# Softmax sums taken over halved keys, and a first convolution computed twice instead of kept

## The chip, the cores and the metric

The kernel runs on one core of a Trainium2 chip. The metric is the device time of one execution in microseconds (us). A core has five engines that run at the same time and wait for each other through semaphores: TensorE (PE in the profile, with its weight loads listed as PEld), VectorE (DVE), ScalarE (ACT), GpSimd (POOL) and SyncE (SP), which here issues the DMA transfers.

## The reference

Two layers are applied to x, four images of 128 channels and 128x128 pixels, all in fp32.

Layer 0 cuts each image into 9x9 overlapping regions of 16x16 pixels with a step of 14. Each region is normalised over the channels and goes through attention with 4 heads of 32 channels; the projected result is added to the region, and overlapping regions are averaged. What follows is a layer norm, a projection to 256 channels, a depthwise 5x5 convolution, a batch norm, two GELUs, a projection back to 128 channels and a residual. For one region and one head:

```
attn = softmax(q @ k.T * hd ** -0.5)     # 256 queries x 256 keys
o    = attn @ v
```

Layer 1 is a block of two 3x3 convolutions with activations and weights quantised to 4 bits:

```
out = act_quant(x)                         # clip to 0..1, round to 15 levels
out = conv3x3(out, weight_quant(w1)); out = batchnorm(out, gamma1, beta1)
out = act_quant(out)
out = conv3x3(out, weight_quant(w2)); out = batchnorm(out, gamma2, beta2)
return out + x
```

A batch norm takes its mean and variance over all four images, so a convolution has to be finished for all of them before any of its results can be normalised.

## The kernel before, in words

**Attention (lines 287 to 705).** A band is one row of 9 regions; there are 4 x 9 = 36 bands and 324 regions. The order of work on PE, ACT and VectorE is written out by hand: these three run their instructions in the order in which the program records them, while GpSimd's and SP's orders come from the scheduler. For region j of a band the loop records `scores(j)`, then `values` of the region before (kept in `last`), then half of the side steps due, then `values_in(j)`, then the other half.

`scores(j)` multiplies keys by queries, with the keys on the partitions (line 561), and takes the exponentials on ACT (line 569). Each of the two tiles `pt` holds two heads and two halves of the keys, 128 keys each, for 256 queries. `values(j)` multiplies them by v and, for the sums, by a matrix of ones; both are accumulated over the two halves (line 615). The reciprocal of the sums (line 628) and the products with it (lines 630, 632) are VectorE's; GpSimd adds the overlapping columns (line 635). An fp32 matmul appears as two rows in the profile, so that one region has 16 rows with v and 16 with ones.

The side steps belong to the band after (normalise and project to q and k: lines 306 to 318 and 382 to 389), to the band before (output projection line 420, residual `xf` line 423, second layer norm, projection line 437) and to the depthwise convolution of an earlier half image (line 496, its copy line 505, its statistics line 507). At a band's start GpSimd averages the overlaps (lines 404, 405, 407), which line 420 then reads. In `normalise`, ACT squares into the tile `sq` (line 308), PE averages it (line 313), and ACT makes `rstd` of it in two steps (lines 315, 316); VectorE multiplies (`xn`, line 318).

**First quantised convolution (lines 800 to 864).** This and the rest is ordered by the scheduler. A block is 4 rows of an image; there are 128. Each block loads the depthwise results `cv` and the residual `xfl` (two blocks ahead), applies batch norm and both GELUs on ACT (lines 841, 846), projects (line 849, four rows on PE), stores the layer's output `id_d`, and quantises it into the padded fp8 image `q1`. `first_conv` then convolves the block before it (line 787, nine matmuls), takes its statistics (line 794) and keeps the result: images 0 to 2 are copied to a tile and written to `c1_d` in memory (lines 829, 831), image 3 is copied to `c1_s` in SBUF.

**Second quantised convolution (lines 865 to 925).** When all statistics are there, a scale and a shift are made from them (on VectorE and, for the power at line 725, GpSimd). Then each block's first result is loaded again (line 881, two blocks ahead) or read from `c1_s`; ACT scales it (line 889), VectorE quantises it (lines 890, 891) into `q2`, which takes the buffers of `q1`, and the second convolution runs for its statistics alone. A last pass computes the second convolution again, scales it (line 918), adds the stored input and writes the output.

Of the kernel before, what the change touches and what calls it, by code (L numbers as in the profile page):

```python
# [8 lines left out]
F32 = mybir.dt.float32  # L9
F8 = mybir.dt.float8e4  # L10
AF = mybir.ActivationFunctionType
ALU = mybir.AluOpType
AX = mybir.AxisListType

P = 128
HEADS = 4
HD = P // HEADS
# [3 lines left out]
NT = RS * RS  # L21
RB = 4
# [19 lines left out]
def layers(  # L42
# [29 lines left out]
    nc = tc.nc  # L72
    B = x.shape[0]
# [14 lines left out]
    ]  # L88
    cv_d = [dram.tile([P // GR, 2 * P, GR * P], F32, name=f"cv_d{b}") for b in range(B)]
    dw_d = dram.tile([NCK, P, 16 * 3 * 32], F32, name="dw_d")  # L90

    c1_d = [dram.tile([P, P * P], F32, name=f"c1_d{b}") for b in range(B - 1)]
    id_d = [dram.tile([P, P * P], F32, name=f"id_d{b}") for b in range(B)]

    def vector(v, name):
# [191 lines left out]
    with ExitStack() as actx:  # L287
# [3 lines left out]
        xp, rp, yp, op = pool("xp", 4), pool("rp", 2), pool("yp", 2), pool("op", 2)  # L291
        y2p, up, cp = pool("y2p", 2), pool("up", 2), pool("cp", 2)
        work, att, attn_t = pool("work", 2), pool("att", 2 if safe else 4), pool("attn_t", 2 if safe else 3)
        small = pool("small", 6)
        ps_s, ps_o, ps_m = (pool(n, k, space=PSUM) for n, k in (("ps_s", 1), ("ps_o", 1), ("ps_m", 3)))

        xb, yr, qs, kr, ob = {}, {}, {}, {}, {}
# [1 line left out]
        def normalise(src, n):  # L299


            held = {}

            def head():
                pc = ps_m.tile([P, 512], F32, name="pm")
                nc.tensor.matmul(pc[:, :n], center, src(), start=True, stop=True)  # L306
                sq = work.tile([P, 512], F32, name="sq")
                nc.scalar.activation(sq[:, :n], pc[:, :n], AF.Square)  # L308
                held["sq"] = sq

            def tail():
                pv = ps_m.tile([P, 512], F32, name="pm")
                nc.tensor.matmul(pv[:, :n], avg, held["sq"][:, :n], start=True, stop=True)  # L313
                rstd = work.tile([P, 512], F32, name="rstd")
                nc.scalar.activation(rstd[:, :n], pv[:, :n], AF.Ln, bias=eps_t)  # L315
                nc.scalar.activation(rstd[:, :n], rstd[:, :n], AF.Exp, scale=-0.5)
                xn = work.tile([P, 512], F32, name="xn")
                nc.vector.tensor_tensor(xn[:, :n], src(), rstd[:, :n], ALU.mult)  # L318
                return xn

            return head, tail
# [209 lines left out]
        def attention(t):  # L531
# [24 lines left out]
            def scores(j):  # L556
# [10 lines left out]
                for p in range(2):  # L567
                    pt = att.tile([P, 2, 2, NT], F32, name="pt")
                    nc.scalar.activation(pt, sc[p], AF.Exp)  # L569
                    S["pt", j].append(pt)  # L570

            def scores_safe(j):
                S["pt", j] = [att.tile([P, 2, 2, NT], F32, name="pt") for p in range(2)]
                qt = attn_t.tile([P, NT], F32, name="rd")
                nc.vector.tensor_copy(
                    qt.rearrange("p (r c) -> p r c", c=RS), queries(j, slice(0, P))
                )
                for h in range(HEADS):
                    hs = slice(h * HD, (h + 1) * HD)
                    sc = ps_s.tile([P, 2, 2, NT], F32, name=f"sc{h % 2}")  # L580
                    for c in range(2):
                        nc.tensor.matmul(
                            sc[:, 0, c, :],
                            qt[hs, c * P : (c + 1) * P], region(kr, j)[hs],
                            start=True, stop=True,
                        )
                    nmax = small.tile([P, 2], F32, name="nmax")
                    nc.vector.tensor_reduce(nmax, sc[:, 0], AX.X, ALU.max, negate=True)
                    pr = attn_t.tile([P, 2, NT], F32, name="pr")
                    den = small.tile([P, 2], F32, name="den")  # L590
                    for c in range(2):
                        nc.scalar.activation(
                            pr[:, c, :], sc[:, 0, c, :], AF.Exp, bias=nmax[:, c : c + 1],
                            accum_out=den[:, c : c + 1],
                        )
                    nc.vector.reciprocal(den, den)
                    for c in range(2):
                        nc.gpsimd.tensor_scalar(
                            pr[:, c, :], pr[:, c, :], den[:, c : c + 1], 1.0, ALU.mult, ALU.mult
                        )  # L600
                    for kc in range(2):
                        for c in range(2):
                            nc.tensor.transpose(
                                sc[:, 1, kc, c * P : (c + 1) * P], pr[:, c, kc * P : (kc + 1) * P], ident
                            )
                    nc.scalar.copy(S["pt", j][h // 2][:, h % 2], sc[:, 1])

            def values(j):
                pt, v = S.pop(("pt", j)), S.pop(("v", j))
                po = ps_o.tile([P, 2, NT], F32, name="po")  # L610
                for m in range(1 if safe else 2):
                    for kc in range(2):
                        for h in range(HEADS):
                            hs = slice(h * HD, (h + 1) * HD)
                            nc.tensor.matmul(  # L615
                                po[hs, m, :], ones if m else v[:, kc, hs], pt[h // 2][:, h % 2, kc, :],
                                start=(kc == 0), stop=(kc == 1),
                            )
                o, po_ = ob[t], po[:, 0, :].rearrange("p (r c) -> p r c", c=RS)
                new = o[:, :, j * STEP + 2 if j else 0 : j * STEP + RS]  # L620
                part = attn_t.tile([P, RS, 2], F32, name="part")
                if safe:
                    nc.vector.tensor_copy(new, po_[:, :, 2 if j else 0 :])
                    if j:
                        nc.vector.tensor_copy(part, po_[:, :, 0:2])
                else:
                    rd = attn_t.tile([P, NT], F32, name="rd")
                    nc.vector.reciprocal(rd, po[:, 1, :])  # L628
                    rd_ = rd.rearrange("p (r c) -> p r c", c=RS)
                    nc.vector.tensor_tensor(new, po_[:, :, 2 if j else 0 :], rd_[:, :, 2 if j else 0 :], ALU.mult)  # L630
                    if j:
                        nc.vector.tensor_tensor(part, po_[:, :, 0:2], rd_[:, :, 0:2], ALU.mult)
                if j:
                    seam = o[:, :, j * STEP : j * STEP + 2]
                    nc.gpsimd.tensor_tensor(seam, seam, part, ALU.add)

            begin()
            return scores_safe if safe else scores, values_in, values

        def beside(t):  # L640

# [37 lines left out]
        with nullcontext() if safe else tc.manual_schedule(engines=MANUAL):  # L679
# [3 lines left out]
                    s()  # L683
            last = None
            for t in range(T):
                scores, values_in, values = attention(t)
                if t + 1 < T:
                    ln1_begin(t + 1)
                side, at = beside(t), 0
                for j in range(NR):  # L690
                    scores(j)
                    if last:
                        last()
                    if j == 0 and t:
                        post_begin(t - 1)
                    for half in range(2):
# [96 lines left out]
    def stats_of(st, n, pc):  # L793
        nc.vector.bn_stats(st[:, n, :], pc.rearrange("p r c -> p (r c)"))  # L794
# [2 lines left out]

    c1_s = q1p.tile([P, P * P], F32, name="c1_s")  # L800
    q1 = [padded(q1p, f"q1_{b}") for b in range(B)]
    with (
        tc.tile_pool(name="ld", bufs=3) as ld,
# [16 lines left out]
            nc.sync.dma_start(out=xf, in_=xf_d[b][:, px])  # L820
            loaded[n] = cv, xf

        def first_conv(n):
            b, k = blocks[n]
            px = slice(k * RB * P, (k + 1) * RB * P)
            pc = conv3x3(q1[b], wq[0], k)
            stats_of(st1, n, pc)
            o = bw.tile([P, RB * P], F32, name="c1") if b < B - 1 else c1_s[:, px]
            nc.scalar.copy(o, pc.rearrange("p r c -> p (r c)"))
            if b < B - 1:  # L830
                nc.sync.dma_start(out=c1_d[b][:, px], in_=o)

        load(0)
        load(1)
        for n, (b, k) in enumerate(blocks):
# [22 lines left out]
                a.rearrange("p (r c) -> p r c", c=P), ROUND, None, ALU.subtract, saturate=False,  # L858
            )
            if k:  # L860
                first_conv(n - 1)
            if k == NBLK - 1:
                first_conv(n)

    sc1, sh1 = batchnorm([st1], 1, ga1, be1, kscale[0], "1")
    nc.vector.tensor_scalar(sc1, sc1, 15.0, None, ALU.mult)
    nc.vector.tensor_scalar(sh1, sh1, 15.0, None, ALU.mult)


    q2 = [padded(q1p, f"q1_{b}") for b in range(B)]  # L870
    ew = ctx.enter_context(tc.tile_pool(name="ew", bufs=3))
    firsts = {}

    def load_first(n):
        b, k = blocks[n]
        px = slice(k * RB * P, (k + 1) * RB * P)
        if b == B - 1:
            firsts[n] = c1_s[:, px]
            return
        firsts[n] = ew.tile([P, RB * P], F32, name="c1l")  # L880
        nc.sync.dma_start(out=firsts[n], in_=c1_d[b][:, px])

    load_first(0)
    load_first(1)
    for n, (b, k) in enumerate(blocks):
        if n + 2 < len(blocks):
            load_first(n + 2)
        a = ew.tile([P, RB * P], F32, name="a")
        nc.scalar.activation(a, firsts.pop(n), AF.Relu, bias=sh1, scale=sc1)
        nc.vector.tensor_scalar(a, a, 15.0, ROUND, ALU.min, ALU.add)  # L890
        nc.vector.tensor_scalar(
            q2[b][:, 1 + k * RB : 1 + (k + 1) * RB, 1 : 1 + P],
# [77 lines left out]
```

## Time and profile before

| what | value |
|---|---|
| three runs | 4054.0, 4057.53 and 4063.75 us; median 4057.53 |
| profiled execution | 4057.53 us; span of its instructions 4055.7 us |
| granted TensorE clock, mean | 0.973 |
| PE busy | 3762.9 us (93%), 35916 rows |
| VectorE busy | 1826.5 us (45%) |
| ScalarE busy | 2326.4 us (57%) |
| GpSimd busy | 384.2 us (9%) |
| DMA | 643.68 MB, 159 GB/s over the span |

The span runs from the first to the last instruction of one profiled execution; its own time has 1.8 us more around it. Busy time is the union of an engine's rows. Matmuls are pipelined: a row lasts from its start to the modelled end of its result, and the next one can start before that. The granted clock is the share of full speed that PE was given. A release, written `<-`, names what ended an engine's idle time.

### The profile page before, as it was taken

To read this page: it belongs to the slowest core of one execution; us is meant where nothing else is said; L and a number is where in the kernel's file an instruction comes from. 1 tells how busy PE (TensorE), PEld (TensorE's weight loads), DVE (VectorE), ACT (ScalarE), POOL (GpSimd) and SP (SyncE) were. 2 spreads that over 40 slices of the span, in tenths; PEclk is the share of its full clock that TensorE was granted. 3 is DMA by queue.
4 is the path that set the end of the run, shared out by engine and by line. 5 is a ranking of instruction groups with operands and counts; after the bars stand their busy time and mean duration, and the time that the engine had idled before them with its cause. 6 is when DMAs were issued, how large, how long until landed. Compare 5 with 4: busy or idle time off the path is not lost.

```text
span 4055.7 us, 87210 instructions
## 1 busy us (share of the span) xinstructions
PE 3762.9 (93%) x35916; PEld 1914.1 (47%) x35916; DVE 1826.5 (45%) x3358; ACT 2326.4 (57%) x3534; POOL 384.2 (9%) x1381
## 2 busy tenths in 40 slices
PE   7699999999999999999999999997688889999999
PEld 5355455555555555555545555553333333334444
DVE  5244444444444444444444444442245555685433
ACT  3367666666666666666666666653156667662233
POOL 0011110111110010111110111100011111100000
PEclk9999999999999999999999999998579999999999
DMA  1223266676656657655666764657888889760487
GB/s 39 108 62 80 73 135 149 146 143 152 148 116 141 148 134 159 150 140 110 150 147 139 160 146 118 144 129 162 182 255 300 295 297 304 231 199 1 137 271 250
DMA packets 782938, 643.68 MB, mean 159 GB/s; under 512 B 572736, under 2 KB 585664, under 8 KB 782528
## 3 DMA queue, kind: packets, MB, share of 16 engines
q1 hardware_dynamic: 782528, 637.98, 60.8%
q8 instruction: 286, 4.69, 0.5%
q14 instruction: 124, 1.02, 0.1%
HBM read 365.07 MB, written 272.76 MB: 157 GB/s over the span
## 4 chain that ended last, share of the span: by engine, by line
PE 76%; DMA 9%; ACT 4%; issue 3%; DVE 3%; POOL 2%; SPq 2%; ACTq 0%; POOLq 0%; DVEq 0%
PE po L615 14%; PE pc L787 12%; PE pm L496 9%; PE sc L561 8%; PE pm L306 6%; PE pm L382 6%; PE pm L313 6%; PE pm L437 5%; DMA cv<-cv_d 3%; PE pm L549 3%; PE pb L849 3%; PE pm L420 2%; PE pw L269 2%; DMA c1l<-c_d 2%; DMA u<-y_d 2%
## 5 line engine op out<-in xcount | busy, mean ns | idle before, releaser
L628 DVE RECIPROCAL rd<-po 128x256 f32<-128x256 f32 x324 | 569.6, 1758 | 633.4 <-PE po L615 633.4
L787 PE MATMUL pc<-q,wq 128*128 128x512 fp8e4 x3456 | 794.5, 382 | 23.3 <-DVE st L794 9.4
L569 ACT ACTIVATE pt<-sc 128x1024 f32<-128x1024 f32 x648 | 627.2, 1019 | 58.0 <-PE sc L561 47.1
L787 PEld LDWEIGHTS <-wq 128*128 128x128 fp8e4 x3456 | 337.4, 98 | 517.5 <-issue 151.6
L496 PE MATMUL pm<-u,w 40*32 40x256 f32 x12288 | 454.6, 410 | 57.4 <-DMA u<-y_d 44.7
L507 DVE BATCH_NORM_STATS2 st<-c 128x6 f32<-128x256 f32 x512 | 181.4, 414 | 469.4 <-ACT c L505 468.9
L561 PE MATMUL sc<-q,kr 32*128 32x256 f32 x5184 | 373.6, 401 | 0.0
L496 PEld LDWEIGHTS pm<-u,w 40*32 40x32 f32 x12288 | 258.7, 112 | 240.8 <-issue 112.2
L505 ACT COPY c<-pm 128x512 f32<-128x512 f32 x256 | 139.0, 588 | 386.8 <-PE pm L496 377.8
L615 PE MATMUL po<-pt,v 128*32 128x256 f32 x5184 | 346.9, 385 | 0.0
L615 PE MATMUL po<-pt,ones 128*32 128x256 f32 x5184 | 339.1, 379 | 0.0
L561 PEld LDWEIGHTS sc<-q,kr 32*128 32x128 f32 x5184 | 233.9, 184 | 218.7 <-issue 181.3
L313 PE MATMUL pm<-sq,avg 128*128 128x512 f32 (+1 forms) x576 | 281.9, 571 | 31.7 <-ACT sq L308 27.0
L443 ACT ACTIVATE y<-pm,bp 128x512 f32<-128x512 f32 (+1 forms) x288 | 183.4, 641 | 222.9 <-PE pm L437 111.9
L849 PE MATMUL pb<-ge,wp 128*128 128x512 f32 x512 | 265.6, 614 | 46.6 <-ACT ge L846 46.5
L382 PE MATMUL pm<-xn,wqkv 128*128 128x512 f32 (+1 forms) x576 | 269.2, 570 | 15.6 <-DVE xn L318 15.6
L437 PE MATMUL pm<-xn,wp 128*128 128x512 f32 (+1 forms) x576 | 268.9, 559 | 5.7 <-DVE xn L318 5.7
L841 ACT ACTIVATE ge<-cv,shift,scale 128x512 f32<-128x512 f32 x256 | 202.8, 844 | 111.2 <-DMA cv<-cv_d 107.2
L308 ACT ACTIVATE sq<-pm 128x512 f32<-128x512 f32 (+1 forms) x288 | 157.2, 546 | 187.8 <-PE pm L306 187.7
L794 DVE BATCH_NORM_STATS2 st<-pc 128x6 f32<-128x512 f32 x256 | 177.8, 696 | 189.3 <-PE pc L787 189.2
L918 ACT ACTIVATE z<-pc,shift,scale 128x512 f32<-128x512 f32 x128 | 99.3, 777 | 269.0 <-PE pc L787 130.1
L315 ACT ACTIVATE rstd<-pm,eps_t 128x512 f32<-128x512 f32 (+1 forms) x288 | 184.3, 640 | 120.3 <-PE pm L313 114.7
(143 smaller groups left out, 4026.0 us busy)
## 6 DMA issues: line engine op xcount, KB each, us to landing
u<-y_d SPq DMA_DIRECT2D x128, 528.0 KB
cv_d<-c SPq DMA_DIRECT2D x512, 128.0 KB
cv<-cv_d SPq DMA_DIRECT2D x128, 512.0 KB
y_d<-y SPq DMA_DIRECT2D x224, 264.0 KB
w<-dw_d SPq DMA_DIRECT2D x64, 768.0 KB
xfl<-xf_d SPq DMA_DIRECT2D x128, 256.0 KB
id_d<-y SPq DMA_DIRECT2D x128, 256.0 KB
idt<-id_d SPq DMA_DIRECT2D x128, 256.0 KB
```

What stands on the lines that cost most here:

```text
L306: nc.tensor.matmul(pc[:, :n], center, src(), start=True, stop=True)
L313: nc.tensor.matmul(pv[:, :n], avg, held["sq"][:, :n], start=True, stop=True)
L382: nc.tensor.matmul(pm[:, : n * P], wqkv[:, m * P : (m + 1) * P], held["xn"][:, : n * P], start=True, stop=True,)
L437: nc.tensor.matmul(pm[:, : n * P], wp0[:, h, :], held["xn"][:, : n * P], start=True, stop=True)
L496: nc.tensor.matmul(pc[half][32 * q : 32 * q + 32, j, :].rearrange("p (g x) -> p g x", g=4), wt[hs, c, s, :], ut[hs, :, c, s : s + 64], sta ...
L561: nc.tensor.matmul(sc[h // 2][:, h % 2, kc, :].rearrange("p (r c) -> p r c", c=RS), region(kr, j)[hs, kc * P : (kc + 1) * P], queries(j, h ...
L569: nc.scalar.activation(pt, sc[p], AF.Exp)
L615: nc.tensor.matmul(po[hs, m, :], ones if m else v[:, kc, hs], pt[h // 2][:, h % 2, kc, :], start=(kc == 0), stop=(kc == 1),)
L628: nc.vector.reciprocal(rd, po[:, 1, :])
L787: nc.tensor.matmul(pc, w[:, t, :], q[:, k * RB + dy : k * RB + dy + RB, dx : dx + P], start=(t == 0), stop=(t == 8),)
L841: nc.scalar.activation(ge[:, h, :].rearrange("p (r c e) -> p r e c", r=RB, e=2), cv[:, h, :].rearrange("p (r e c) -> p r e c", r=RB, e=2), ...
L849: nc.tensor.matmul(pb, wp2[:, h, :], ge[:, h, :], start=(h == 0), stop=(h == 1))
```

## The change

In attention, VectorE adds the exponentials of the two halves of the keys (`halves`, into new tiles `sm0` and `sm1` in a pool of one buffer each), and the product with ones runs over the sums: 4 fp32 matmuls for each region in place of 8. `halves(j)` is recorded behind `values` of the region before. To make room, `rstd` takes the buffer of `sq`.

In layer 1 the first convolution's results are not kept. The first pass takes their statistics alone (`first_stats`), and the second pass convolves each block again, from `q1`, straight in front of the scaling on ACT, which now reads PSUM. `q2` has buffers of its own, since `q1` is still needed.

```diff
-    c1_d = [dram.tile([P, P * P], F32, name=f"c1_d{b}") for b in range(B - 1)]
...
-                rstd = work.tile([P, 512], F32, name="rstd")
+                rstd = held["sq"]
...
+            def halves(j):
+                S["sm", j] = []
+                for p in range(2):
+                    sm = sums.tile([P, 2, NT], F32, name=f"sm{p}")
+                    pt = S["pt", j][p]
+                    nc.vector.tensor_tensor(sm, pt[:, :, 0, :], pt[:, :, 1, :], ALU.add)
+                    S["sm", j].append(sm)
...
-                for m in range(1 if safe else 2):
-                    for kc in range(2):
-                        for h in range(HEADS):
-                            hs = slice(h * HD, (h + 1) * HD)
-                            nc.tensor.matmul(
-                                po[hs, m, :], ones if m else v[:, kc, hs], pt[h // 2][:, h % 2, kc, :],
-                                start=(kc == 0), stop=(kc == 1),
-                            )
+                for kc in range(2):
+                    for h in range(HEADS):
+                        hs = slice(h * HD, (h + 1) * HD)
+                        nc.tensor.matmul(
+                            po[hs, 0, :], v[:, kc, hs], pt[h // 2][:, h % 2, kc, :],
+                            start=(kc == 0), stop=(kc == 1),
+                        )
+                if not safe:
+                    sm = S.pop(("sm", j))
+                    for h in range(HEADS):
+                        hs = slice(h * HD, (h + 1) * HD)
+                        nc.tensor.matmul(
+                            po[hs, 1, :], ones, sm[h // 2][:, h % 2, :], start=True, stop=True
+                        )
...
                     if last:
                         last()
+                    halves(j)
...
-        def first_conv(n):
+        def first_stats(n):
             b, k = blocks[n]
-            px = slice(k * RB * P, (k + 1) * RB * P)
-            pc = conv3x3(q1[b], wq[0], k)
-            stats_of(st1, n, pc)
-            o = bw.tile([P, RB * P], F32, name="c1") if b < B - 1 else c1_s[:, px]
-            nc.scalar.copy(o, pc.rearrange("p r c -> p (r c)"))
-            if b < B - 1:
-                nc.sync.dma_start(out=c1_d[b][:, px], in_=o)
+            stats_of(st1, n, conv3x3(q1[b], wq[0], k))
...
-    q2 = [padded(q1p, f"q1_{b}") for b in range(B)]
+    q2p = ctx.enter_context(tc.tile_pool(name="q2p", bufs=1))
+    q2 = [padded(q2p, f"q2_{b}") for b in range(B)]
...
     for n, (b, k) in enumerate(blocks):
-        if n + 2 < len(blocks):
-            load_first(n + 2)
+        pc = conv3x3(q1[b], wq[0], k)
         a = ew.tile([P, RB * P], F32, name="a")
-        nc.scalar.activation(a, firsts.pop(n), AF.Relu, bias=sh1, scale=sc1)
+        nc.scalar.activation(a, pc.rearrange("p r c -> p (r c)"), AF.Relu, bias=sh1, scale=sc1)
```

More of the change, by code (lines that the diff above doesn't have):

```diff
@@ L293, in layers @@
         work, att, attn_t = pool("work", 2), pool("att", 2 if safe else 4), pool("attn_t", 2 if safe else 3)
-        small = pool("small", 6)
+        small, sums = pool("small", 6), pool("sums", 1)
         ps_s, ps_o, ps_m = (pool(n, k, space=PSUM) for n, k in (("ps_s", 1), ("ps_o", 1), ("ps_m", 3)))
@@ L637, in attention @@
             begin()
-            return scores_safe if safe else scores, values_in, values
+            if safe:
+                return scores_safe, lambda j: None, values_in, values
+            return scores, halves, values_in, values
         def beside(t):
@@ L685, in layers @@
             for t in range(T):
-                scores, values_in, values = attention(t)
+                scores, halves, values_in, values = attention(t)
                 if t + 1 < T:
@@ L796, in layers @@
     blocks = [(b, k) for b in range(B) for k in range(NBLK)]
-    c1_s = q1p.tile([P, P * P], F32, name="c1_s")
     q1 = [padded(q1p, f"q1_{b}") for b in range(B)]
@@ L860, in layers @@
             if k:
-                first_conv(n - 1)
+                first_stats(n - 1)
             if k == NBLK - 1:
-                first_conv(n)
+                first_stats(n)
     sc1, sh1 = batchnorm([st1], 1, ga1, be1, kscale[0], "1")
@@ L867, in layers @@
     nc.vector.tensor_scalar(sh1, sh1, 15.0, None, ALU.mult)
-    q2 = [padded(q1p, f"q1_{b}") for b in range(B)]
+    q2p = ctx.enter_context(tc.tile_pool(name="q2p", bufs=1))
+    q2 = [padded(q2p, f"q2_{b}") for b in range(B)]
     ew = ctx.enter_context(tc.tile_pool(name="ew", bufs=3))
[L872 to L884, printed above, removed]
     for n, (b, k) in enumerate(blocks):
-        if n + 2 < len(blocks):
-            load_first(n + 2)
+        pc = conv3x3(q1[b], wq[0], k)
         a = ew.tile([P, RB * P], F32, name="a")
-        nc.scalar.activation(a, firsts.pop(n), AF.Relu, bias=sh1, scale=sc1)
+        nc.scalar.activation(a, pc.rearrange("p r c -> p (r c)"), AF.Relu, bias=sh1, scale=sc1)
         nc.vector.tensor_scalar(a, a, 15.0, ROUND, ALU.min, ALU.add)
```

## The prediction

> **What bounds the kernel now.** I read the page first (which engine, which slices), then busy time by stage, because the change touches three stages with different limits, then the timeline inside each. The page's shares say that TensorE (PE) leads nearly everywhere:
>
> ```profile
> PE 3762.9 (93%) x35916; PEld 1914.1 (47%) x35916; DVE 1826.5 (45%) x3358; ACT 2326.4 (57%) x3534; POOL 384.2 (9%) x1381
> ...
> PE 76%; DMA 9%; ACT 4%; issue 3%; DVE 3%; POOL 2%; SPq 2%; ACTq 0%; POOLq 0%; DVEq 0%
> ```
>
> The stages, from the busy times in stretches (PE, PEld, DVE, ACT, POOL busy us, then granted clock, DMA share, GB/s):
>
> ```profile
> 169.00:2771.00 2602.00, 2512.15 (x29724) 1347.43 (x29724) 1139.31 (x1784) 1648.04 (x2589) 282.19 (x1176) 1.00 0.58 132
> 2771.00:2978.00 207.00, 135.70 (x1987) 61.54 (x1976) 56.57 (x176) 36.58 (x62) 5.40 (x23) 0.59 0.82 171
> 2978.00:3397.00 419.00, 373.36 (x1237) 151.15 (x1237) 218.26 (x382) 295.33 (x386) 66.06 (x114) 0.99 0.90 299
> 3397.00:3520.00 123.00, 120.74 (x428) 53.19 (x428) 73.41 (x131) 96.07 (x126) 21.31 (x36) 1.00 0.83 274
> 3520.00:3528.00 8.00, 0.00 (x0) 0.00 (x0) 6.14 (x13) 2.30 (x4) 2.10 (x5) 0.69 0.43 149
> 3528.00:3798.00 270.00, 259.73 (x1159) 113.50 (x1160) 176.66 (x384) 99.59 (x126) 0.00 (x0) 0.98 0.31 91
> ```
>
> Row 1 is attention with its side work: PE is busy 97% of 2602 us, so PE slots are the currency there. Row 2 is the last depthwise unit, waiting for DMA; the change leaves it alone. Rows 3 and 4 are the first quantised convolution: 96 blocks (images 0 to 2) while DMA moves 299 GB/s, then 32 blocks (image 3) with less traffic and PE busy 98%. Row 5 is the batch-norm step with PE idle. Row 6 is the second convolution's statistics. The 258 us after it (second convolution again, output) are not touched.
>
> **Slots.** A PE row's duration is latency; what it costs is the distance from start to start, which the timeline gives:
>
> ```profile
> 1503.45 1.07 PE L615 MATMUL po<-pt,v 128*32 128x256 f32 x16
> ...
> 1504.34 1.05 PE L615 MATMUL po<-pt,ones 128*32 128x256 f32 x16
> 1505.31 0.73 PEld L382 LDWEIGHTS pm<-xn,wqkv 128*128 128x128 f32 x4 [0.41 <-issue]
> ...
> 3506.90 2.12 PE L787 MATMUL pc<-q,wq 128*128 128x512 fp8e4 x9
> 3508.86 1.02 PE L849 MATMUL pb<-ge,wp 128*128 128x512 f32 x2
> 3509.71 0.81 PE L787 MATMUL pc<-q,wq 128*128 128x512 fp8e4 x3
> ```
>
> Sixteen rows of the value product hold PE from 1503.45 to 1504.34: 0.89 us, or 0.222 us for each four that run side by side. The ones product takes 0.97 us: the same 0.89 and 0.09 for the change back to 128-column weights. Nine fp8 matmuls take 1.96 us (0.217 each), two fp32 ones 0.85 us.
>
> [...]here, after 8.5 us idle at 3519.6, thirteen fp8 matmuls start 0.43 us apart, so a long gap costs about 2.8 us more, while single waits near 1 us in row 6 are followed by 0.22 spacing. [...]line 318 (two SBUF inputs, 128x512) shows 693. [...]line 407, 0.382 us at the median, took 0.692 where it fell beside line 318.
>
> **The change, part by part.** The sum stands against the profiled execution: 4057.5 us, its span 4055.7 and 1.8 around it; that execution is also the median of the three runs.
>
> *1. Ones product over half the keys.* Of 16 rows per region 8 go: two groups of four, 0.444 us. The 0.09 for the weight change stays. 324 regions x 0.444 = **-143.9 us** of PE slots. PE waits in this stage in few places:
>
> ```profile
> PE pm L420 <- POOL ob L407: 46.2, 31, 4.5
> PE pm L313 <- ACT sq L308: 23.6, 35, 0.7
> PE pm L496 <- ACT y L443: 7.9, 29, 0.4
> PE pm L382 <- DVE xn L318: 6.5, 6, 1.8
> ```
>
> In none of them does a ones product lie between the producer's start and the wait, so its removal does not lengthen them.
>
> *2. Two adds on VectorE per region.* 648 x 0.69 us = 447 us on an engine busy 1139 of 2602: 1586 of about 2500, 63%, not the bound. The adds are issued behind the previous region's reciprocal and products, so they start when "part" (line 632) ends, some 3 us after the ones rows end; their sums are read by the next region's product, a region (about 8 us) later. What queues behind them on VectorE: xf (line 423), xn (line 318), the statistics (line 507). I shifted each in the trace's own order by the 1.4 us, where VectorE had no idle time to take it up, and compared with the time from its end to the matmul that reads it (xf to line 306: 2.9 us or more in nine of ten; xn to line 382 or 437: 2.6 to 3.8 mostly). Only about a dozen of some 425 overrun: **+10 us**.
>
> At a band's start there is no such slack. GpSimd's chain there (seam add line 635 0.25, then 404, 405, 407: 0.72, 0.41, 0.38 us) ends in the 46 us wait of line 420 above, and the two adds now run at the same moment[...]. Bounds: 0 (GpSimd always first) and 1.4 us x 36 bands = 50. VectorE needs no hop between engines after "part" and GpSimd does, so I take about 1 us each: **+35 us**. Attention together: -144 + 10 + 35 = **-99 us** (-134 to -75). Taking rstd into sq's buffer moves nothing: Ln waits for the matmul that read sq anyway.
>
> *3. First convolution, statistics only.* Gone: 128 copies on ACT (0.57 us, ACT not the bound), 96 writes of 256 KB on SP's queue, each waiting for its copy ahead of the next loads. Images 0 to 2 take 415/96 = 4.32 us a block from the first projection at 2982, with 1280 KB moved; image 3, which wrote nothing, keeps PE's own pace: 2 x 0.85 + 1.96 = 3.66 us. With 1024 KB a block DMA needs 286 GB/s at that pace, less than the 299 it has shown. So PE sets it: 96 x (4.32 - 3.67) = **-62 us** (-45 if DMA still binds at times, -64).
>
> *4. First convolution again.* 1152 more matmuls at 0.216: 249 us, all in row 6, where PE is already 96% busy. Before, from the scale's readiness (3526.1) to the last statistics (3797.5): 271 us. After: 18 of the 2304 matmuls run in row 5's gap, the other 2286 take 494; 2 us to the first, 2.8 at half clock, 1 at the end; 500 us without waits, **+229**. Waits come on top. In the built order the last three matmuls of the second convolution of a block need the next block's quantised rows, and only eight matmuls (six of that convolution, two of the recompute after next) stand between the recompute's last matmul and them: 8 x 0.216 = 1.73 us of cover. The chain they wait for: 0.16 drain, 0.04 to ACT, 0.78 (line 918 reading PSUM), 0.03, 0.42 and 0.42 on VectorE with 0.03 between, 0.1 to PE: 2.0 us. The links as they stand in the trace:
>
> ```profile
> 3526.28 2.22 ACT L889 ACTIVATE a<-c1l,shift,scale 128x512 f32<-128x512 f32 x3 [5.29 <-DVE shift L867]
> ...
> 3527.13 0.43 DVE L890 TENSOR_SCALAR a<-a 128x512 f32<-128x512 f32 x1 [0.93 <-ACT a L889]
> 3527.59 0.43 DVE L891 TENSOR_SCALAR q<-a 128x512 fp8e4<-128x512 f32 x1
> ...
> 3528.17 22.19 PE L787 MATMUL pc<-q,wq 128*128 128x512 fp8e4 x90 [8.53 <-DVE q L891]
> ```
>
> Short by 0.28 us, about 125 times: +35 (0 to 60). The statistics stand behind that quantising on VectorE and end 0.9 us after their own matmuls, before ACT delivers the next block: no further wait. Stage: **+264 us**. The loads of the kept results (96 x 256 KB) go; they caused waits already inside the 271. GpSimd's border memsets for four new tiles (1.5 us each) stand ahead of the batch-norm power on its queue; they can start when the last blocks drain, and end about when it is due: 0 to +2.
>
> **Sum:** -99 - 62 + 264 = +103: 4160 us.
>
> **Rivals.**
> *No wait in the recompute stage* (ACT's and VectorE's links shorter, or weights pulled ahead): 4160 - 35 = 4125; with nothing given back in attention, 4080. For it: the shortfall is only 0.28 us. Against: every link is measured. 0.17.
> *Attention gives back more.* If VectorE's adds and GpSimd's copies hold each other in all 324 regions, 0.25 us each, +81: 4240. For it: ACT at 63% and VectorE at 63% leave less idle time to absorb delays. Against: the slack above. 0.10.
> *Statistics ahead in VectorE's queue*: if a quantising finds the previous block's statistics running, 0.69 us per block, +86: 4246. Against: 1.5 us between them. 0.06.
> *Not slower.* One mechanism: PE's weight loads run ahead of every wait and seam, so that the 0.09 us weight change after the ones product goes with it (324 x 0.09 = -29), and the recompute never waits: -144 - 29 - 64 + 229 = -8, 4050. It decides from 0.53 us saved a region on, and only if the chain fits into 1.73 us. Nothing shows a hidden weight change now. 0.04.
> That the recompute is not carried out can be excluded: the built order has nine matmuls of each convolution for every block.
>
> **Numbers.** The likeliest case has 0.63 and by itself 4130 to 4190. For 8 in 10 I add most of the first rival and the start of the second: 4100 to 4210. A difference within 0.2% (8 us) is what a measurement of this kernel can't tell from none. PE's own count, with no wait added, is already about +20 (-144 - 64 + 229), so both other outcomes need a mechanism not seen: slower 0.96, same 0.02, faster 0.02.
>
> **What would show it.** Attention 2602 to about 2500 us with PE still near 97% busy; VectorE some 450 us busier; line 407's successor releasing PE about 80 us instead of 46. Image 0 to 2 at 3.67 us a block with no write of kept results. The recompute stage 535 us with about 0.3 us of PE idle time a block released by the quantising. A region that shortens by less than 0.3 us, or a recompute stage under 505 us, would prove steps 2 or 4 wrong.

## The result, and the profile after

The changed kernel takes 4188.03 us (median of 4 runs, 4184.51 to 4199.35) against 4055.77 us for the kernel before beside it: a ratio of 1.0328, 95% interval 1.0303 to 1.0353. It is slower by about 132 us. The prediction had 4160 us and a range of 4100 to 4210.

First the page of the changed kernel, the shares of the engines and of the chain that ended last. PE and VectorE are each busier than before, by 128 and 420 us, and PE's share of the chain has risen to 81%.

```profile
PE 3891.1 (93%) x34476; PEld 1956.9 (47%) x34476; DVE 2246.1 (54%) x4006; ACT 2272.0 (54%) x3406; POOL 492.0 (12%) x1381
...
PE 81%; ACT 5%; DVE 4%; DMA 4%; POOL 2%; issue 2%; SPq 1%; ACTq 0%; DVEq 0%; POOLq 0%
```

Next the busy times of the same stages in the changed kernel (columns as in the prediction):

```profile
169.00:2704.00 2535.00, 2395.76 (x27136) 1272.75 (x27130) 1540.03 (x2432) 1648.07 (x2588) 389.89 (x1174) 0.99 0.62 135
2704.00:2911.00 207.00, 136.75 (x1976) 63.02 (x1968) 56.25 (x175) 39.57 (x64) 7.84 (x30) 0.58 0.84 178
2911.00:3387.00 476.00, 470.79 (x1655) 208.90 (x1656) 287.74 (x510) 336.08 (x382) 80.47 (x132) 1.00 0.85 279
3387.00:3396.00 9.00, 6.16 (x29) 2.55 (x27) 6.33 (x11) 0.09 (x1) 6.41 (x17) 1.00 0.01 3
3396.00:3926.00 530.00, 519.65 (x2291) 222.62 (x2292) 199.18 (x385) 99.33 (x128) 0.00 (x0) 0.99 0.00 1
```

Row by row against the kernel before: attention is 67 us shorter, but PE is now busy 94.5% of it and no longer 97%. POOL (GpSimd) has the same instructions there, but its busy time rose from 282 to 390 us; that is the first sign that something holds it. The first quantised convolution has one pace of 3.67 us a block from beginning to end and takes 478 us from its first projection to its last statistics, where it took 538. The second pass moves nothing by DMA and has doubled: 530 us from the first scaling on ACT to the last statistics, where it took 271. So -67 - 60 + 259, with 4 to 5 us less around them, makes the 127 us between the two spans.

The waits of PE in the attention stage (waiting line, what it waited for, total us, times, longest):

```profile
PE pm L418 <- POOL ob L405: 82.1, 35, 5.2
PE pm L311 <- ACT sq L306: 23.6, 35, 0.7
PE pm L494 <- ACT y L441: 16.7, 52, 0.4
...
PE pm L304 <- DVE xf L421: 4.8, 9, 0.6
```

Lines have moved by two: 418 is the output projection, 405 the last of GpSimd's steps at a band's start. That wait has grown from 46 to 82 us. Why, the durations of GpSimd's instructions show (line, operation, count: duration min/median/max in ns, first and last start), with VectorE's adds in the last row, from the same kernel:

```profile
L648 POOL TENSOR_TENSOR ob<-ob,part x288: 249/628/710, 186.0 to 2707.1; 128x32 f32<-128x32 f32 x144
L402 POOL TENSOR_TENSOR ob<-ob x32: 722/1050/1057, 281.5 to 2707.4; 128x256 f32<-128x256 f32 x32
L405 POOL TENSOR_SCALAR ob<-ob x36: 379/693/718, 222.4 to 2708.7; 128x224 f32<-128x224 f32 x32, 128x256 f32<-128x256 f32 x4
L576 DVE TENSOR_TENSOR sm<-pt x648: 679/682/909, 170.5 to 2701.3; 128x512 f32<-128x512 f32 x162
```

Before, the same three GpSimd steps had medians of 254, 725 and 382 ns. They are 0.37, 0.33 and 0.31 us longer, 1.01 us together for a band. One band's start in the changed kernel shows what holds them, and what PE does after it:

```profile
603.45 1.34 DVE L576 TENSOR_TENSOR sm<-pt 128x512 f32<-128x512 f32 x2
...
603.61 0.63 POOL L648 TENSOR_TENSOR ob<-ob,part 128x32 f32<-128x32 f32 x1 [2.19 <-DVE part L645]
...
604.32 1.05 POOL L402 TENSOR_TENSOR ob<-ob 128x256 f32<-128x256 f32 x1
...
605.52 0.88 DVE L316 TENSOR_TENSOR xn<-xt,sq 128x512 f32<-128x512 f32 x1 [0.74 <-POOL ob L402]
605.94 0.69 POOL L405 TENSOR_SCALAR ob<-ob 128x224 f32<-128x224 f32 x1
```

```profile
606.69 1.13 PE L418 MATMUL pm<-ob,wo 128*128 128x512 f32 x2 [2.19 <-POOL ob L405]
607.65 1.57 PE L380 MATMUL pm<-xn,wqkv 128*128 128x512 f32 x2
609.15 2.09 PE L559 MATMUL sc<-q,kr 32*128 32x256 f32 x16
```

The same place in the kernel before:

```profile
616.60 1.13 PE L420 MATMUL pm<-ob,wo 128*128 128x512 f32 x2 [1.19 <-POOL ob L407]
617.56 1.02 PE L382 MATMUL pm<-xn,wqkv 128*128 128x512 f32 x2
618.51 1.15 PE L561 MATMUL sc<-q,kr 32*128 32x256 f32 x16
```

The first two GpSimd steps run beside the adds. The third runs beside `xn` (line 316), which now starts 0.42 us ahead of it; in the kernel before, `xn` runs beside this step as well in 27 bands, but in 26 of them starts 0.28 us behind it, and the step keeps its 0.38 us. So in 26 ordinary bands PE waits 2.2 us in place of 1.2 us, which is 26 us of the 36; 2 us are short waits that were not there before, and 7 us lie in the five longest waits.

The wait has a second price. The product with 16 rows at 609.15 takes 2.09 us, where the same product takes 1.15 us in the kernel before. The granted clock behind the wait is half (columns as above):

```profile
608.00:611.40 3.40, 3.40 (x22) 1.43 (x24) 0.61 (x1) 0.81 (x2) 0.00 (x0) 0.50 0.86 214
```

Beside the 26 waits of 1.2 us in the kernel before, no record of the clock shows half; beside the 26 waits of 2.2 us in the changed kernel, 11 do. Of the five longest waits, three have half clock beside them before and all five after. In all of attention, PE is at half clock for 14 us before and for 72 us after.

In the second pass PE shows hardly any wait as such: a row there lasts 0.38 us (median), and the next starts 0.216 us after it, so that the rows overlap and cover a short stop. The weight loads show it. The timeline of the changed kernel, weight loads on PE, then VectorE's quantising of a block:

```profile
3600.41 3.78 PEld L803 LDWEIGHTS <-wq 128*128 128x128 fp8e4 x18 [0.34 <-issue]
...
3604.53 3.78 PEld L803 LDWEIGHTS <-wq 128*128 128x128 fp8e4 x18 [0.34 <-issue]
3608.66 0.31 PEld L803 LDWEIGHTS <-wq 128*128 128x128 fp8e4 x2 [0.34 <-issue]
```

```profile
3604.05 0.43 DVE L887 TENSOR_SCALAR q<-a 128x512 fp8e4<-128x512 f32 x1
...
3608.17 0.43 DVE L887 TENSOR_SCALAR q<-a 128x512 fp8e4<-128x512 f32 x1
```

Eighteen loads, the two convolutions of a block, then a stop that ends 0.05 us after a quantising ends (3604.48, 3608.60). The period is 4.12 us where 18 x 0.216 = 3.89 would do.

### The profile page after: what moved, and what is told of

Same layout as the page of the kernel before. It is cut to its first block, busy times and chain, and to the rows that moved or that the text cites. A ratio compares the mean times of both kernels' runs of the same rounds, so it can differ in the third digit from the quotient of the medians.

```text
span 4182.7 us, 84939 instructions
## 1 busy us (share of the span) xinstructions
PE 3891.1 (93%) x34476; PEld 1956.9 (47%) x34476; DVE 2246.1 (54%) x4006; ACT 2272.0 (54%) x3406; POOL 492.0 (12%) x1381
## 4 chain that ended last, share of the span: by engine, by line
PE 81%; ACT 5%; DVE 4%; DMA 4%; POOL 2%; issue 2%; SPq 1%; ACTq 0%; DVEq 0%; POOLq 0%
PE pc L803 19%; PE pm L494 9%; PE sc L559 8%; PE po L621 7%; PE pm L380 6%; PE pm L304 6%; PE pb L858 5%; PE pm L311 5%; PE pm L435 5%; PE po L629 3%; PE pm L547 3%; PE pm L418 3%; ACT a L885 2%; PE pw L267 2%; DMA y_d<-y 1%
## 5 line engine op out<-in xcount | busy, mean ns | idle before, releaser
L803 PE MATMUL pc<-q,wq 128*128 128x512 fp8e4 x4608 | 1052.7, 380 | 13.7 <-issue 4.6
L803 PEld LDWEIGHTS <-wq 128*128 128x128 fp8e4 x4608 | 448.2, 97 | 648.9 <-issue 158.8
L576 DVE TENSOR_TENSOR sm<-pt 128x512 f32<-128x512 f32 x648 | 430.6, 705 | 6.5 <-ACT pt L567 6.5
L559 PE MATMUL sc<-q,kr 32*128 32x256 f32 x5184 | 382.7, 409 | 0.1
L885 ACT ACTIVATE a<-pc,shift,scale 128x512 f32<-128x512 f32 x128 | 99.4, 777 | 442.7 <-PE pc L803 426.1
L380 PE MATMUL pm<-xn,wqkv 128*128 128x512 f32 (+1 forms) x576 | 279.8, 590 | 14.7 <-DVE xn L316 14.4
L858 PE MATMUL pb<-ge,wp 128*128 128x512 f32 x512 | 252.4, 597 | 10.6 <-ACT ge L855 10.6
L648 POOL TENSOR_TENSOR ob<-ob,part 128x32 f32<-128x32 f32 x288 | 161.7, 561 | 829.9 <-DVE part L645 828.1
L547 PEld LDWEIGHTS pm<-wqkv,yr 128*128 128x128 f32 x1296 | 193.6, 191 | 122.3 <-issue 116.3
```

The lines of the kernel that those rows point to most:

```text
L380: nc.tensor.matmul(pm[:, : n * P], wqkv[:, m * P : (m + 1) * P], held["xn"][:, : n * P], start=True, stop=True,)
L547: nc.tensor.matmul(pv[:, c, :], region(yr, j)[:, c * P : (c + 1) * P], wqkv[:, 2 * P :], start=True, stop=True)
L559: nc.tensor.matmul(sc[h // 2][:, h % 2, kc, :].rearrange("p (r c) -> p r c", c=RS), region(kr, j)[hs, kc * P : (kc + 1) * P], queries(j, h ...
L576: nc.vector.tensor_tensor(sm, pt[:, :, 0, :], pt[:, :, 1, :], ALU.add)
L803: nc.tensor.matmul(pc, w[:, t, :], q[:, k * RB + dy : k * RB + dy + RB, dx : dx + P], start=(t == 0), stop=(t == 8),)
L858: nc.tensor.matmul(pb, wp2[:, h, :], ge[:, h, :], start=(h == 0), stop=(h == 1))
```

## The experiments

Unless it says otherwise, a kernel here keeps the first convolution's results as the kernel before does. Line numbers of these kernels lie one above those of the changed kernel (output projection 419, GpSimd's last step at a band's start 406).

**First set: each part alone, and the attention part taken in two.**

The attention part alone has the hunks of `attention`, `normalise` and the loop, and none of layer 1. The convolution part alone has the rest.

> The attention part of the change alone (adds on VectorE, product with ones over the sums, rstd in sq's buffer); the first convolution keeps its results as before. Theory: the two parts don't touch each other. The changed kernel's attention ended 67 us earlier than before (2704 against 2771 us), so this kernel takes 4056 - 67 = 3989 us, 3975 to 4000: faster. Rival: the parts are coupled (SBUF layout, order made by the scheduler), and the sum of the two kernels with one part each misses the changed kernel by more than 15 us.

> The convolution part of the change alone (first pass for statistics only, first convolution computed again); attention as before. Theory of independent parts: first pass 60 us shorter, second pass 259 us longer, 4056 + 199 = 4255 us, 4245 to 4265. Rival of coupled parts: outside that.

Measured: 3989.15 us, ratio 0.9843 (0.9827 to 0.9859); and 4250.98 us, 1.0499 (1.0479 to 1.0519). The parts are independent: -1.57% and +4.99% make +3.42%, and the whole change has +3.28% with an interval of 0.25% to both sides. The convolution part's stages are 478 us and 530 us, those of the changed kernel. The attention part by itself is a gain.

To price the adds alone, the product stays over all keys:

```diff
-                    sm = S.pop(("sm", j))
-                    for h in range(HEADS):
-                        nc.tensor.matmul(po[hs, 1, :], ones, sm[h // 2][:, h % 2, :], start=True, stop=True)
+                    S.pop(("sm", j))
+                    for kc in range(2):
+                        for h in range(HEADS):
+                            nc.tensor.matmul(po[hs, 1, :], ones, pt[h // 2][:, h % 2, kc, :],
+                                             start=(kc == 0), stop=(kc == 1))
```

> Before, with the adds on VectorE put in at the same place and the product with ones still over all keys (the sums are written and not read). It prices the adds alone. Theory G (give-back): the halved product saves its half of the slots, 144 us, and the adds give about 70 us back, some 36 of it where GpSimd's chain at the start of a band is held by the adds: 4056 + 70 = 4126 us, 4105 to 4135. Rival H: the adds cost next to nothing, and the halved product saves only some 68 us of slots: 4056 to 4066 us.

To price the halved product alone, `halves(j)` is left out:

```diff
-                            po[hs, 1, :], ones, sm[h // 2][:, h % 2, :], start=True, stop=True
+                            po[hs, 1, :], ones, pt[h // 2][:, h % 2, 0, :], start=True, stop=True
...
-                    halves(j)
```

> Before, with the product with ones over the first half of the keys alone and no adds: the second half of the keys is left out of the sums. It prices the halved product alone. Theory G: 324 x 0.444 us less, 4056 - 144 = 3912 us, 3905 to 3925. Rival H: about 3988 us.

Measured: with the adds 4116.58 us, 1.0166 (1.0149 to 1.0184), attention 67 us longer; with the halved product 3925.08 us, 0.9691 (0.9675 to 0.9707), attention 129 us shorter. Theory G holds against H, with a smaller gain than its 144 us: 3925 us is at the upper end of its range, while the kernel before, run beside it, took 4050 us and not 4056. The difference of the two, 62 us, is near the 67 us of the attention part.

**Second set: where the adds stand, and the cover in the second pass.**

The adds of a band's first region move behind its side steps:

```diff
-                    halves(j)
+                    if j:
+                        halves(j)
...
+                    if j == 0:
+                        halves(j)
                     last = lambda j=j, values=values: values(j)
```

> The attention part alone (3989 us), with the adds of a band's first region recorded behind that region's side steps instead of ahead of them; all other adds stay. GpSimd's chain at a band's start does not wait for the adds on VectorE's queue in either place[...]: PE's wait for that chain goes back from 84 to about 48 us, 3989 - 36 = 3953 us, 3945 to 3965. Rival, queue: the growth of that wait comes from VectorE's longer queue or from the shorter ones product in front of it, and the time stays at 3980 to 3992 us.

Measured: 3946.16 us, 0.9728 (0.9703 to 0.9753), attention 41 us shorter than in the attention part alone. For GpSimd's steps the expectation holds: two of its band-start steps, the first two rows below, have their old durations (0.72 and 0.38 us) once no add runs beside them. The third row is the seam add of every region, of which only one in eight is affected by this edit, and which still takes 0.63 us. In the queue, `xn` at 605.52 above had not waited for the adds, which had ended 0.74 us earlier: ACT's second step for `rstd` (line 314) ended at 605.44, and GpSimd's second step, which the profile names, at 605.37. But PE's wait fell by 25 us (79 to 54 within attention) and not by the 36 us of the expectation; nearly all the rest of the 41 us is the clock, as the table at the end of this section shows.

```profile
L403 POOL TENSOR_TENSOR ob<-ob x32: 721/723/725, 287.0 to 2668.9; 128x256 f32<-128x256 f32 x32
L406 POOL TENSOR_SCALAR ob<-ob x36: 377/379/404, 227.8 to 2670.1; 128x224 f32<-128x224 f32 x32, 128x256 f32<-128x256 f32 x4
L649 POOL TENSOR_TENSOR ob<-ob,part x288: 247/627/807, 190.0 to 2668.5; 128x32 f32<-128x32 f32 x144
```

Now all adds behind all side steps:

```diff
-                    halves(j)
...
                         if half == 0:
                             values_in(j)
+                    halves(j)
                     last = lambda j=j, values=values: values(j)
```

> The attention part alone (3989 us), with the adds of every region recorded behind all its side steps. [...]GpSimd's chain is free as above (-36 us), and xf and xn no longer stand behind the adds (some -20 us): 3933 us, 3925 to 3955. Rival: the adds, now last on VectorE's queue before the next region, come late for the product with ones or delay the next reciprocal; PE shows waits of line 630 for the adds, and the time is above 3960 us.

Measured: 4174.47 us, 1.0292 (1.0266 to 1.0318). The rival came true, and far beyond its bound. PE's waits in this kernel's attention, which lasts to 2891 us, and below them one region in its timeline:

```profile
PE po L630 <- DVE sm L577: 90.6, 194, 1.8
PE pm L419 <- POOL ob L406: 45.6, 31, 4.5
```

```profile
1512.77 0.69 DVE L317 TENSOR_TENSOR xn<-xt,sq 128x512 f32<-128x512 f32 x1 [1.26 <-issue]
...
1513.16 1.07 PE L622 MATMUL po<-pt,v 128*32 128x256 f32 x16
...
1513.38 1.76 DVE L577 TENSOR_TENSOR sm<-pt 128x512 f32<-128x512 f32 x2
...
1514.12 0.63 PE L630 MATMUL po<-sm,ones 128*32 128x256 f32 x4
...
1515.19 0.62 PE L630 MATMUL po<-sm,ones 128*32 128x256 f32 x4 [0.45 <-DVE sm L577]
1515.75 0.30 PEld L436 LDWEIGHTS pm<-xn,wp 128*128 128x128 f32 x2 [0.41 <-issue]
```

The adds now stand behind xn, which starts 0.09 us after ACT's second step for `rstd` has ended (1512.68), so they start when the product with v is already running. The ones product falls into two groups of four rows, each waiting for its own add, and holds PE for 1.63 us (1514.12 to 1515.75) in place of about 0.56. By start-to-start times the ones rows and the step onto them hold PE 260 us longer over the stage than in the attention part alone. The list of waits shows 91 us of it, because it counts idle time alone. In return PE's wait for GpSimd's chain is back at 46 us, as in the kernel before.

In the second pass of the changed kernel the second convolution goes two blocks behind the recompute:

```diff
-        if k:
-            stats_of(st2, n - 1, conv3x3(q2[b], wq[1], k - 1))
+        if k > 1:
+            stats_of(st2, n - 2, conv3x3(q2[b], wq[1], k - 2))
         if k == NBLK - 1:
+            stats_of(st2, n - 1, conv3x3(q2[b], wq[1], k - 1))
             stats_of(st2, n, conv3x3(q2[b], wq[1], k))
```

> The changed kernel (4188 us in its own runs, 1.0328 of before) with the second convolution of the second pass two blocks behind the recompute instead of one, so that 24 matmuls stand between the recompute of a block and the matmuls that need its quantised rows, in place of 8. Chain theory: the 0.22 us of extra spacing a block (115 starts at 0.44 us) disappear, 26 us less: ratio to before 1.026 to 1.028. Rival: the extra spacing belongs to the change between the two sets of weights, which comes as often here, and the ratio stays at 1.032 to 1.034.

Measured: 4156.44 us, 1.0251 (1.0224 to 1.0279); the pass takes 498 us in place of 530. The chain theory holds: the starts 0.44 us apart are gone from the trace though the weights change as before, block by block. The weight loads of this kernel, where the other stopped after each 18:

```profile
3599.70 8.35 PEld L803 LDWEIGHTS <-wq 128*128 128x128 fp8e4 x39
```

**Third set: the best place.**

```diff
                         if half == 0:
+                            halves(j)
                             values_in(j)
```

> The attention part alone, with the adds of every region recorded between the two halves of its side steps, ahead of values_in. Theory[...]: GpSimd's chain at a band's start is free of the adds (-36 us), the xf and xn of the first half no longer stand behind them, and some 3 us stay to the next product with ones: 3989 - 36 - 10 = 3943 us, 3925 to 3955. Rival (late adds): the adds already stand behind a VectorE operation that waits for ACT, PE waits for the sums as in the kernel with the adds last, and the time is above 3965 us.

The other kernel has `if j:` before this call, and `halves(0)` last in its region.

> As the kernel with the adds between the two halves, but those of a band's first region behind all its side steps. Theory: if at a band's start the middle is still within GpSimd's chain, this one is 10 to 20 us faster than the former; if not, it is the same or up to 5 us slower, because these adds then come late for the next product (1.5 us in 36 bands).

Measured (5 runs each): 3934.58 us, 0.9704 (0.9682 to 0.9727), and 3929.98 us, 0.9695 (0.9671 to 0.9719). Both are faster than the attention part alone (0.9843). Against the kernel whose band-start adds alone were moved (0.9728) the intervals overlap; in the profiled executions attention is 8 and 19 us shorter than there. Between the two the difference is inside the intervals. The trace of the first one shows GpSimd's band-start steps at 724 and 379 ns already, so its chain is free of the adds there too, and a place of their own for the adds at a band's start is not shown to gain anything. PE's longest waits in the last one's attention stage:

```profile
PE pm L419 <- POOL ob L406: 51.4, 31, 4.8
PE pm L312 <- ACT sq L307: 23.6, 35, 0.7
PE pm L495 <- ACT y L442: 8.2, 29, 0.5
```

Nothing in it waits for the sums. Attention takes 2471.5 us (first to last row of the `po` product), and the kernel with the halved product and no adds takes 2468.7: at this place 648 adds, 424 us of VectorE, cost 3 us in these two executions, and the two ratios (0.9695 and 0.9691) are the same within their intervals.

**Where the adds cost time.** Attention of eight kernels, from the first to the last row of the `po` product, in us. The third column is PE's idle time in it, the fourth the part of this that ends in the output projection, the fifth the time for which PE is busy at half clock:

| kernel | attention | PE idle | before the output projection | PE busy at half clock |
|---|---|---|---|---|
| before | 2598 | 90 | 46 | 11 |
| adds, product over all keys | 2665 | 130 | 74 | 68 |
| halved product, no adds | 2469 | 94 | 51 | 24 |
| attention part alone | 2532 | 136 | 79 | 68 |
| whole change | 2532 | 139 | 82 | 62 |
| adds later at a band's start | 2490 | 112 | 54 | 31 |
| adds between the halves, last at a band's start | 2471 | 95 | 51 | 24 |
| adds later everywhere | 2720 | 180 | 46 | 14 |

At half clock the 16 rows at 609.15 above held PE for 2.02 us, until 611.17, where those at 618.51 in the kernel before held it for 1.09 us, until 619.60. So half of the last column is an estimate of what the clock costs. With it the prices close: the adds alone add 40 us of idle time and 28 us of clock, and attention is 67 us longer. Moving them at a band's start takes away 23 and 18 us, and attention is 41 us shorter. Only the last kernel does not close in this way, because there the late sums also cost time that is not idle.

## Why the prediction was right, and where it was off

*Slots of the ones product (-144).* Right in kind. The trace has 139 us less for the ones rows; the factor 0.444 for two groups of four was 0.432. The stage without adds is 129 us shorter. The prediction held that no wait grows with the shorter product; PE's idle time is 4 us longer, and some 7 us go to half clock (half of 24 less 11).

*The adds (+10 queue, +35 at a band's start).* As a forecast of PE's idle time this was near: it grew by 49 us, of which 36 lie before the output projection, 9 before line 494 (for ACT's y) and 5 before line 304 (for xf). The cause of the 36 was right in part. The adds do start ahead of GpSimd's chain: `part` ends at 603.53, they start at 603.45 and the seam add at 603.61. Beside them two of GpSimd's steps take longer, 0.70 us of the 1.01; the other 0.31 come from `xn` starting ahead of the third (the prediction's own example, line 407 beside line 318, was the one band of 27 where `xn` began first). Only 26 bands have the extra 1.0 us, and the halved product without any adds already has 51 us in place of 46. So the closeness of 82 us to "about 80" is in part luck. The waits for y and xf go back once the adds stand between the two halves of the side steps, where the seam adds on GpSimd (line 649) also have their old median of 253 ns. Whether y's wait comes through GpSimd or through VectorE's queue was not separated: both were relieved together.

*The term that was missing.* The prediction had priced the half clock for the second pass and put it at nothing in attention. There it costs about 26 us (half of 62 less 11), because half clock followed a wait of 2.2 us in 11 of 26 bands. With it the sum for attention is -139 + 49 + 26 = -64 us, where -66 were measured. The forecast was -99 us, with a range of -134 to -75, so this part fell outside its range, and that is nearly the whole miss of the total. By the prediction's own sign, a region that shortens by less than 0.3 us, step 2 was wrong: 67 us in 324 regions are 0.21 us. Nor did PE stay near 97% busy. The total came out inside its range because the other two parts were within 5 us.

*First pass (-62).* -60 us. PE sets the pace at 3.67 us a block (busy 471 of 476 us), and DMA at 279 GB/s does not.

*Second pass (+264).* +259 us: 229 us of slots and an extra 0.22 us in 115 blocks, where 0.28 in 125 was forecast. The experiment with a longer cover takes 32 us out of the pass, 25 of them in those 115 starts, and so shows that the extra was this wait; the pass without it (498 us) is what the slots make (500).

*The unlikely rivals.* That VectorE's adds and GpSimd hold each other in every region came true on one side: 251 of the 288 seam adds run beside an add and take 0.63 us in place of 0.25, but the adds' median stays 0.68 us, and away from a band's start PE's idle time rose by 14 us only, not by the rival's 81. Statistics ahead of the quantising did not occur (no 0.69 us step in the period), nor did a stream without any wait. What was forecast as the most certain point, that PE's own count alone is on the slow side (+20 us), holds as a sum: with each part at the best that a run of the full computation showed, the stages make -127 - 60 + 227 = +40 us. No run had all three together.

## What to carry to other kernels

Price a trade between engines by slots first, then look at what each new instruction holds beside its own queue, and at PE's clock behind a longer wait (half in 11 of 26 bands after 2.2 us, in none of 26 after 1.2 us): here two adds a region were nearly free at one place in VectorE's order, cost 63 to 67 us at another and about 250 us at a third (attention 2720 us, against 2469 without adds). Ask of a result that is computed again whether its stage has room on that engine: here the copies and writes that the recompute saved were worth 60 us in a stage with PE 89% busy, and the stage that took the matmuls, 96% busy before, grew by 259 us. And measure the parts of a change by themselves; the whole was 3.3% slower with a 1.6% gain inside it.

## What was not expected of the hardware

The VectorE add of two SBUF operands (0.68 us) lengthened the small GpSimd instruction beside it by more than that instruction's own length: 254 to 628 ns for 32 columns. Its end goes with the end of the add: the seam add ends 0.11 us, and the 256-column add 0.58 us (0.579 to 0.586 in 27 bands), after the VectorE add that was running when it began (medians), and both are 0.14 us less than what each takes alone.

A PE wait of 2.2 us, with one of 0.7 us shortly ahead of it, was followed by 3.4 us at half clock in 11 of 26 bands, and a wait of 1.2 us in the same place in none of 26.

In the kernel with all adds behind the side steps, the list of waits understated operands that came late. Split in two by late sums, the eight rows of the ones product held PE for 1.63 us instead of about 0.56, 1.07 us more, while the list shows 0.45 us of idle time ahead of the second four.
